# One 2 MB transfer in place of four of 512 KB for each input tile of a graph-layer kernel

## The chip, the core and the metric

The kernel runs on one core of a Trainium2 chip. The profile names the core's engines: PE (matrix multiplication, with its weight loads in a row of their own, PEld), DVE and ACT (elementwise work), POOL (elementwise work and indirect transfers) and SP (which here only issues transfers). Transfers between the chip's memory (DRAM in the code) and the core's on-chip memory are moved by 16 DMA engines. The metric is the device time of one execution in microseconds (us), first to last. Differences of up to about 0.2% (3.9 us here) are what repeated measurements of this kernel cannot tell from nothing.

## The reference: what is computed

For each of 32 batches, x is a 512 x 1024 matrix (channels by nodes) in 32-bit floats. Layer 0 is an attention over the nodes with rank-one scores, layer 1 a plain product with the same 512 x 512 matrix `adj`; each has a residual and a normalization over the last axis:

```python
q = jnp.einsum('c,bcn->bn', wq, x)
k = jnp.einsum('c,bcn->bn', wk, x)
scores = q[:, None, :] + k[:, :, None]
att = jax.nn.softmax(jnp.where(scores > 0, scores, 0.01 * scores), axis=-1)
agg = jnp.einsum('bcn,bmn->bcm', x, att)
x = _layernorm(x + relu(jnp.einsum('oc,bcm->bom', adj, agg) + bm[None, :, None]), axis=-1)
out = _layernorm(x + jnp.einsum('bnf,nm->bmf', x, adj * adj) + bias, axis=-1)
```

## The kernel before, in words

One batch's x is held on chip as a tile of 128 partitions by 4 chunks by 1024 nodes: chunk c holds channels 128c to 128c+127, one to a partition, 4 KB each. `load(b)` (lines 84 to 88) takes a tile from the pool `xp`, which has four buffers, and fills it with four transfers on SP's queue, one for each chunk, of 128 rows of 4 KB. Since there are four buffers, the tile of batch b takes the place of batch b-4, which is still an operand in layer 1 of that batch until its last matrix product and its last DVE combination are done; the first of the four transfers waits for both.

The first reader of a new tile is `parts(b)` (line 247), the products with the two vectors wq and wk. It runs on PE as 16 matrix instructions, chunk by chunk, each with 256 nodes:

```python
for c in range(CT):
    for g in range(CT):
        nc.tensor.matmul(s.ps[32 * g : 32 * g + 32, :], wqk[:, c, :],
            xts[b][:, c, g * Q : (g + 1) * Q], start=(c == 0), stop=(c == CT - 1))
```

The first four of them need chunk 0 alone, the next four chunk 1, and so on. In the profile these are the rows `qk_ps L247`, counted as 32 because each instruction is recorded in two passes. What follows for a batch: the two vectors go to DRAM and come back as a broadcast row (`q_row<-part`, `qb<-q_row`); DVE and ACT count ranks and signs of q against it (`rk` on line 308, `ct` on line 323); PE multiplies x by `adj` (`z_ps` on line 346, and `z_sum_ps` and `z_pair_ps` on line 390, where a two-level scheme saves products); POOL scatters the rows of the product in the order of q to DRAM (`sorted_z`, line 451, eight scatters a batch); they come back (`tab<-sorted_z`, line 470), DVE and ACT make running sums of them, which go out as a table (`table<-tab`, line 553); POOL gathers a row of the table for each node (`got<-table`, line 563); PE turns these (`agg_ps`, line 609), DVE adds the residual into the x tile (line 617), ACT normalizes it, and layer 1 multiplies it (`sum_ps` and `pair_ps`, lines 667 and 702), after which the result is normalized and stored (`out_dram<-g`, line 777).

The order on each engine is written out by hand as a list of words, each a step with its batch: `ld.1` is `load` of the next batch, `pa.1` its `parts`. There is a head for the first batches, a loop that is repeated five times, and a tail. The loop touches five batches at a time, from the next one back to the third before. In the loop, PE's steps between the last product that reads the old tile in its buffer (`12.-3.0`, the pair_ps product of line 667 with S) and `pa.1` are four quarter products (`Y.-3.0`, `Y.-3.1`, `21.-3.0`, `21.-3.1`) and the small `cu.-1` (`carry_ps_True`, line 509). SP issues 16 transfers a batch in the order of the list, each when what it waits for is there: four of x, four of the result, two of `tab`, two of `table`, and four small or broadcast ones. Behind the x transfers in SP's order stands a store of a result chunk. Completion is told through eight semaphores for SP's transfers, taken in turn, so that a transfer also waits for the one eight places before it.

Of the kernel before, what the change touches and what calls it, by code (L numbers as in the profile page):

```python
# [42 lines left out]
P = 128  # L43
# [6 lines left out]
def adj_resnorm_kernel(  # L50
# [10 lines left out]
    nc = tc.nc  # L61
    B, C, N = x.shape
    CT = C // P
# [19 lines left out]

    def load(b):
        t = xp.tile([P, CT, N], F32, tag="x", name=f"x_{b}")
        for c in range(CT):
            nc.sync.dma_start(out=t[:, c, :], in_=x[b, c * P : (c + 1) * P, :])
        xts[b] = t


# [16 lines left out]
    for h in range(2):  # L107
        nc.scalar.dma_start(
            out=room[3 - 3 * h : 6 - 3 * h, 0, :],
            in_=bias[h * H : (h + 1) * H].partition_broadcast(3),  # L110
# [665 lines left out]
    def store(b, m):  # L776
# [5 lines left out]
    ops = {  # L782
        "ldw": adj_load, "wt": adj_turn, "wc": adj_copy_odd, "wd": adj_copy_even, "R": adj_sums,
        "ld": load, "pa": parts, "pc": parts_copy, "co": cols, "cc": cols_copy, "ro": row,
        "tb": top, "tp": top_end, "qw": row_out, "rk": rank, "re": rank_end, "ct": count, "ce": count_end,
        "we": weights_exp, "oq": own_q, "z": product, "zc": product_copy, "sc": scatter,
# [497 lines left out]
```

## Time and profile before

| What | Value |
|---|---|
| median of 3 runs | 1942.26 us (1938.29 to 1942.53) |
| the profiled execution, its own time | 1942.71 us |
| span in its profile | 1940.9 us |
| PE busy | 97% of the span |
| DVE, ACT, POOL busy | 88%, 76%, 46% |
| DMA | 558.05 MB, mean 288 GB/s |
| x transfers | 128 of 512 KB, 0.43 us of SP each (median) |
| granted clock of PE, mean | 0.993 |

The shares are of the span, which runs from the first instruction to the last; the execution's own time is 1.8 us longer. A wait in the profile is named by the instruction that waited and by what ended the wait. The chain is the sequence of work that ended last, followed back from the end: what lengthens a piece of it lengthens the execution. Of the DMA engines the profile has packets (here a packet is mostly one row of a transfer) with queue, start and size: q1 is SP's queue and q0 POOL's.

### The profile page before, as it was taken

To read this page: it belongs to the slowest core of one execution; us is meant where nothing else is said; L and a number is where in the kernel's file an instruction comes from. 1 tells how busy PE (TensorE), PEld (TensorE's weight loads), DVE (VectorE), ACT (ScalarE), POOL (GpSimd) and SP (SyncE) were. 2 spreads that over 40 slices of the span, in tenths; PEclk is the share of its full clock that TensorE was granted. 3 is DMA by queue.
4 is the path that set the end of the run, shared out by engine and by line. 5 is a ranking of instruction groups with operands and counts; after the bars stand their busy time and mean duration, and the time that the engine had idled before them with its cause. 6 is when DMAs were issued, how large, how long until landed. Compare 5 with 4: busy or idle time off the path is not lost.

```text
span 1940.9 us, 23403 instructions
## 1 busy us (share of the span) xinstructions
PE 1887.8 (97%) x7073; PEld 1072.0 (55%) x7073; DVE 1704.6 (88%) x2746; ACT 1483.5 (76%) x2663; POOL 897.2 (46%) x1074
## 2 busy tenths in 40 slices
PE   7988999999999999999999999999999999999897
PEld 3654555555555555566555566555565555554443
DVE  6897899998899889989988989988998989889973
ACT  3566677878778777778787778787777787877786
POOL 5263435335434345454456454455443355445531
PEclk9999999999999999999999999999999999999899
DMA  6577788677888687877787887777888677887862
GB/s 250 197 290 271 286 309 339 253 294 282 313 310 315 252 309 270 331 307 291 290 306 280 317 311 304 277 299 286 308 312 310 262 291 300 308 320 279 331 245 95
DMA packets 147446, 558.05 MB, mean 288 GB/s; under 512 B 19653, under 2 KB 19793, under 8 KB 139129
## 3 DMA queue, kind: packets, MB, share of 16 engines
q1 hardware_dynamic: 89936, 354.40, 48.4%
q0 software_dynamic: 57344, 202.15, 27.6%
q8 instruction: 56, 0.92, 0.2%
q14 instruction: 70, 0.57, 0.1%
q10 hardware_dynamic: 40, 0.02, 0.0%
HBM read 287.08 MB, written 269.42 MB: 287 GB/s over the span
## 4 chain that ended last, share of the span: by engine, by line
PE 78%; DMA 8%; DVE 7%; issue 2%; ACT 2%; POOL 2%; SPq 0%; POOLq 0%; DVEq 0%; ACTq 0%
PE z_ps L346 19%; PE sum_ps L667 18%; PE pair_ps L667 10%; PE z_sum_ps L390 9%; PE z_pair_ps L390 7%; PE pair_ps L702 5%; PE agg_ps L609 4%; DMA table<-tab 3%; PE qk_ps L247 3%; DMA tab<-sorted_z 2%; DVE tab L538 2%; PE carry_ps_True L509 1%; PE carry_ps_False L509 1%; DMA x<-in_x_dram 1%; DMA sorted_z<-zt,to 1%
## 5 line engine op out<-in xcount | busy, mean ns | idle before, releaser
L563 POOL DMA_INDIRECT got<-table,of x256 | 302.3, 1181 | 568.8 <-DMA table<-tab 260.6
L346 PE MATMUL z_ps<-adj_t,x 128*128 128x512 f32 x1088 | 486.9, 594 | 1.4 <-DVE qkc L267 1.1
L451 POOL DMA_INDIRECT sorted_z<-zt,to x256 | 314.0, 1226 | 176.7 <-issue 73.9
L308 DVE SCALAR_TENSOR_TENSOR junk_v<-qb,qkc,tie 128x1024 uint8<-128x1024 f32 x256 | 329.8, 1288 | 10.0 <-DMA qb<-q_row 6.4
L346 PEld LDWEIGHTS z_ps<-adj_t,x 128*128 128x128 f32 x1088 | 202.3, 190 | 225.5 <-issue 212.4
L323 ACT ACTIVATE junk_s<-qb,qkc 128x1024 uint8<-128x1024 f32 x256 | 293.4, 1146 | 19.7 <-DMA qb<-q_row 14.3
L667 PE MATMUL sum_ps<-zt,S 128*128 128x512 f32 x512 | 236.1, 593 | 3.1 <-DVE zt L651 1.4
L585 ACT ACTIVATE got<-got,w 128x512 f32<-128x512 f32 x256 | 172.6, 718 | 42.2 <-DVE w L580 41.8
L590 DVE SCALAR_TENSOR_TENSOR got<-got,w 128x512 f32<-128x512 f32 x256 | 185.6, 746 | 12.0 <-ACT got L585 11.8
L491 DVE SCALAR_TENSOR_TENSOR tab<-tab,ac 128x514 f32<-128x514 f32 x192 | 144.6, 753 | 49.8 <-ACT tab L486 29.2
L617 DVE SCALAR_TENSOR_TENSOR x<-agg_ps,small,x 128x1024 f32<-128x1024 f32 x128 | 163.1, 1280 | 23.9 <-PE agg_ps L609 23.6
L600 ACT ACTIVATE junk<-g,tv 128x1024 uint8<-128x1024 f32 x128 | 146.9, 1148 | 32.9 <-DVE g L722 26.4
L501 DVE SCALAR_TENSOR_TENSOR tab<-tab,ac 128x513 f32<-128x513 f32 x224 | 167.5, 748 | 2.6 <-ACT tab L499 1.9
L667 PEld LDWEIGHTS sum_ps<-zt,S 128*128 128x128 f32 x512 | 96.5, 190 | 121.6 <-issue 105.8
L753 POOL TENSOR_SCALAR tv<-tv 128x1 f32<-128x1 f32 x124 | 53.1, 428 | 238.5 <-ACT junk L600 230.5
L774 ACT ACTIVATE g<-g,nb,tv 128x1024 f32<-128x1024 f32 x124 | 151.0, 1237 | 7.3 <-POOL nb L764 7.2
L600 ACT ACTIVATE junk<-x,tv 128x1024 uint8<-128x1024 f32 x128 | 146.9, 1148 | 12.2 <-DVE x L617 9.9
L538 DVE TENSOR_TENSOR tab<-tab,carry 128x2052 f32<-128x2052 f32 x64 | 146.2, 2291 | 4.7 <-ACT carry L516 4.7
L635 ACT ACTIVATE x<-x,tv 128x1024 f32<-128x1024 f32 x128 | 139.3, 1141 | 0.5
L609 PEld LDWEIGHTS agg_ps<-ident,got 128*128 128x128 f32 x1024 | 116.4, 141 | 36.2 <-issue 24.9
L609 PE MATMUL agg_ps<-ident,got 128*128 128x128 f32 x1024 | 129.4, 274 | 2.7 <-DVE g L722 2.0
L667 PE MATMUL sum_ps<-x,adj 128*128 128x512 f32 x256 | 123.3, 605 | 7.4 <-ACT x L635 7.4
(144 smaller groups left out, 3281.5 us busy)
## 6 DMA issues: line engine op xcount, KB each, us to landing
table<-tab SPq DMA_DIRECT2D x64, 2056.0 KB
tab<-sorted_z SPq DMA_DIRECT2D x64, 1028.0 KB
x<-in_x_dram SPq DMA_DIRECT2D x128, 512.0 KB
out_dram<-g SPq DMA_DIRECT2D x128, 512.0 KB
qb<-q_row SPq DMA_DIRECT2D x32, 512.0 KB
sorted_z<-zt,to POOLq DMA_INDIRECT x256, 5.0
got<-table,of POOLq DMA_INDIRECT x256, 8.0
adj_in<-in_adj_dram SPq DMA_DIRECT2D x1, 1024.0 KB
```

What stands on the lines that cost most here:

```text
L308: nc.vector.scalar_tensor_tensor(s.junk, s.qb, s.q[:, j : j + 1], tie[:, at : at + N], ALU.subtract, ALU.is_gt, accum_out=s.rank[:, j : j ...
L323: nc.scalar.activation(junk, s.qb, AF.Sign, bias=s.k[:, j : j + 1], accum_out=s.sign[:, j : j + 1])
L346: nc.tensor.matmul(s.z[j], xt[:, c, j * P : (j + 1) * P], adj_t[:, c, :], start=(c == 0), stop=(c == CT - 1),)
L390: nc.tensor.matmul(ps, a[:, i, k * P : (k + 1) * P], v[:, i, :], start=start and i == 0 and (k == 0 or bank == 1), stop=(i == 1), skip_gro ...
L451: nc.gpsimd.indirect_dma_start(out=sorted_z[b % 2][:, :], out_offset=bass.IndirectOffsetOnAxis(ap=s.to[:, j : j + 1], axis=0), in_=zt[:, j ...
L538: nc.vector.tensor_tensor(v, v, c, ALU.add)
L563: nc.gpsimd.indirect_dma_start(out=s.got[:, j, :], out_offset=None, in_=table[b % 2][:, :], in_offset=bass.IndirectOffsetOnAxis(ap=s.of[:, ...
L585: nc.scalar.activation(down, down, AF.Copy, scale=s.w[:, 1, j : j + 1])
L590: nc.vector.scalar_tensor_tensor(up, up, s.w[:, 0, j : j + 1], down, ALU.mult, ALU.add)
L600: nc.scalar.activation(junk, t, AF.Square, bias=v[0][:, i : i + 1], scale=-float(N), accum_out=v[1][:, i : i + 1],)
L609: nc.tensor.transpose(s.agg[o][:, j * P : (j + 1) * P], s.got[:, j, o * P : (o + 1) * P], ident)
L667: nc.tensor.matmul(ps, a[:, k, g * P : (g + 1) * P], v[:, k, :], start=False, stop=(k == 1), skip_group_check=first is None,)
```

## The change

Each x tile is filled by one transfer of 2 MB. The tile, its place, the rows of 4 KB and the order of all other steps stay; the transfer has 128 partitions by 4 rows, and there is one completion in place of four. SP issues 13 transfers a batch in place of 16.

```diff
     def load(b):
         t = xp.tile([P, CT, N], F32, tag="x", name=f"x_{b}")
-        for c in range(CT):
-            nc.sync.dma_start(out=t[:, c, :], in_=x[b, c * P : (c + 1) * P, :])
+        nc.sync.dma_start(out=t, in_=x[b].rearrange("(c p) n -> p c n", p=P))
         xts[b] = t
```

## The prediction

> **What bounds the kernel now.** I read the page first. PE is busy nearly all of the span, so only what makes PE wait can move the time. Then the rows by stretches, for the period of the middle batches.
>
> ```profile
> span 1940.9 us, 23403 instructions
> PE 1887.8 (97%) x7073; PEld 1072.0 (55%) x7073; DVE 1704.6 (88%) x2746; ACT 1483.5 (76%) x2663; POOL 897.2 (46%) x1074
> ```
> ```profile
> 934.20:992.43 58.23, 58.23 (x223) 33.67 (x222) 53.07 (x88) 46.76 (x84) 29.36 (x33) 1.00 0.79 299
> 992.43:1050.66 58.23, 58.23 (x223) 33.68 (x222) 52.54 (x86) 46.46 (x84) 29.71 (x33) 1.00 0.80 299
> ```
>
> The columns of the second fence are stretch, length, busy time of PE, PEld, DVE, ACT and POOL, granted clock, DMA share, GB/s. A batch takes 58.23 us there and PE has no gap at full clock: whatever is added to PE's order in this stretch (batches 14 to 25) is added to the time in full.
>
> Third, the order of time around one x load, SP's rows and then PE's.
>
> ```profile
> 934.20 1.77 SPq L87 DMA_DIRECT2D x<-in_x_dram  x4
> 941.15 0.34 SPq L777 DMA_DIRECT2D out_dram<-g  x1
> ```
> ```profile
> 932.67 1.45 PE L667 MATMUL pair_ps<-x,S 128*128 128x512 f32 x3
> 933.96 3.60 PE L667 MATMUL sum_ps<-zt,S 128*128 128x512 f32 x8
> 937.40 3.59 PE L667 MATMUL sum_ps<-zt,adj 128*128 128x512 f32 x8
> 940.83 1.03 PE L509 MATMUL carry_ps_True<-end,before 128*128 128x257 f32 x4
> 941.79 1.93 PE L247 MATMUL qk_ps<-x,wqk 128*32 128x256 f32 x32
> ```
>
> The load is issued when PE ends the last product with the old tile (934.1). PE then has three more steps, and 7.59 us after the first issue (941.79 - 934.20) it starts on the new tile. So this load is not early: PE ties both ends, 7.59 us apart, and the margin does not grow if PE is late.
>
> Fourth, the DMA view: SP's packets from the issue to 941.79, and to 942.4.
>
> ```profile
> q1 hardware_dynamic: 567, 2.07, 82.4%
> ```
> ```profile
> q1 hardware_dynamic: 576, 2.10, 77.1%
> ```
>
> Four loads are 576 packets: 512 rows of 4 KB (2.10 MB), and 64 more, which I take for completions. When PE starts qk_ps, 9 packets have not even begun; the last begins between 942.2 and 942.4. PE does not wait, since chunk 0 is long there and chunk 3 is wanted only after three quarters of 1.93 us, at 943.2. Where the last chunk is really late, the chain shows it.
>
> ```profile
> 408.85 8.04 DMA x<-in_x_dram
> 416.89 0.04 issue
> 416.94 0.64 PE qk_ps L247 x8
> ```
>
> There the last transfer lands at 416.89, the last quarter of qk_ps follows; the view with 576 packets begun is reached between 416.3 and 416.5, so landing comes some 0.4 us after the last packet begins (0.2 to 0.4 by the same reading at 298.86).
>
> **The change part by part.**
>
> Removed: three issues of about 0.43 us a batch. SP issues next a store at 941.15, which waits for ACT, 5 us after; the 1.3 us saved are idle time of SP, and worth nothing. If that cover went, SP would be early, which costs nothing either. With 13 transfers a batch, each still waits for the completion of the one eight places before, now further back in work: no wait is added. In the compiled order nothing else moves on any engine.
>
> Moved: the first four instructions of qk_ps now wait for the whole tile. Queued behind them is all of PE's order, with z_ps next; ACT's copy of qk_ps waits for them, and the row q with it. The price of a batch is (landing of the whole) - (start of qk_ps), where the old order had no wait.
>
> When does one transfer of 2 MB land? No row has it. The nearest in time and rows is the last of the four old ones. It is the same 512 rows on the same queue, and the engines, not the issues, set their pace: issues are 0.47 us apart, 512 KB at the 418 GB/s of a full microsecond (937.20 to 938.20) are 1.25. From one side: in the quickest steady load (817.73) all 576 have begun 7.27 us after the issue, so it lands at 7.7; if one transfer spared the start-up of the later three it could end some 0.4 earlier. From the other: one transfer of 1 MB with four rows a partition (tab, 1433.86) lands 5.42 us after its issue; less 2.6 for its bytes at 400 GB/s leaves 2.8, and 2.8 + 5.2 is 8.0, 0.3 later. The far rows are the 2056 KB writes of the table, 7.6 to 12.1 us in the chain. I take "the same as the last of four", as the nearest, and keep -0.4 to +0.3 for the range. In most batches two scatters of POOL run beside the load and hold it up; they stay.
>
> By the same reading for batches 14 to 25, all packets have begun 1.0, 0, 0.6, 0.6, 0.4, 0.8, 0.4, 0.4, 1.0, 0.8, 0.4, 0.2 us after the start of qk_ps (steps of 0.2): 6.6. With 0.3 for the landing (0.4 less half a step) in eleven and 0.1 in one, 6.6 + 3.4 = 10.0 us, 0.8 a batch.
>
> The early batches: batch 4 0.3, but PE waits 0.9 us some 25 us later for a chain that came off DVE before, so 0; batch 5 0.6 + 0.3 = 0.9; batch 7 0.2; batches 6 and 8 wait for the last chunk today, and there the loss is the three quarters of qk_ps that were done before, 1.93 - 0.64 = 1.29 each. Together 3.7. In batches 9 to 13, 26 to 28 and 30 PE has other work ahead of qk_ps (8.1 to 12.7 us) and all x packets are out: 0. Batches 29 and 31: 575 and 572 packets begun, 0.5 to 0.7 each, 1.3.
>
> The head: today the fourth transfer of x_0 waits 2.5 us for a completion semaphore (SP's waits), is issued at 4.68, and adj behind it at 5.05. Both go out by about 1.7 now. qk_ps of batch 0 ends at 10.45 in the chain; with the whole tile landing 7.7 us after 0.79 and 1.93 of work it is 10.4, so nothing there; but adj is out of the way of x_1 and of the broadcast row behind it, on which DVE waits at 20.9. Between 0 and -1.5; I take -0.7.
>
> Sum: 10.0 + 3.7 + 1.3 - 0.7 = 14.3. Some of the 5 us outside the steady stretch will vanish in gaps that PE has anyway (DVE's chains do not move with the last stall): -1.3. That is +13 on the profiled execution's 1942.71 (span 1940.9 and 1.8 around it), 1955.7; the median of the runs is 0.45 lower, so 1955.3 us, 0.7% slower; a change within 0.2% (3.9 us) could not be told from none.
>
> For the size of a transfer, the trace's rows are 418 GB/s while the 512 KB pieces flow and 7.7 us at best to the landing of the last; by them the sum is the +13 above. The Trainium skill, "DMA: Bandwidth & Descriptors", section "Anatomy of one DMA — SWDGE (gpsimd) path", gives one transfer a fixed 2.0 us and its bytes at 436 GB/s, fitted on POOL's path; that makes an estimate of 6.8 us for 2.10 MB, by which the load would be hidden and the sum about 0. For the number of transfers, the row is the start of qk_ps at 941.79 with 9 packets still to begin. Against this change speaks the page "Perfetto Trace Analysis", section "DMA Optimizations": splitting transfers may let some work start sooner, above all where DMA engines idle (here their share is 0.79); by it one transfer can only lose, and the sum is above 0.
>
> **The rivals.**
> 1. The load is hidden, and the time is the same. It needs the 2 MB to land by +7.59, 0.5 to 1.3 us sooner than the last chunk does in eleven of the twelve steady batches. For it: fewer completions and one start-up, 0.4 at most by the rows above. Time: 14.3 falls to about 0 to 3, 1942 to 1945.
> 2. Faster. If every load, those beside scatters too, lands before qk_ps is reached, the waits on x vanish as well (PE and PEld on DMA x, 1.3 + 4.0 = 5.3 us in all) and the head gives 0.7: -6, 1936. It decides at landings 1.3 us earlier than now; no row has such a gain.
> 3. The four-row form is slow: landing 1 us later than the last chunk. Then the 19 batches that stall pay 1 us more each and some of the others begin to, +33 to +35: about 1976. For it only the 0.3 of the tab row.
> 4. Absorbed: DVE and ACT (88% and 76%) use the stall and PE gains it back at other waits. Against it: PE has no other gap in the steady stretch. If half of the steady 10 and all the rest is gained back, 1947.
>
> **How the numbers follow.** Forecast 0.64 (1948 to 1964: landing -0.4 makes about +6, +0.3 about +19), rival 1 0.14, rival 2 0.05, rival 3 0.09, rival 4 0.08. The range leaves out rival 2 and part of rival 1 below, most of rival 3 above: 1944 to 1969. Slower by over 0.2% (beyond 1946.1): 0.64 + 0.09 + most of rival 4 = 0.80; same 0.15; faster 0.05.
>
> **What would show it.** In the profile after: waits of qk_ps L247 on DMA x, some 25 of 0.2 to 1.3 us, where 9 are now; a steady period of about 59.1 in place of 58.23, with PE's gap at qk_ps alone; the x issue as one row of some 0.4 us; the same mean GB/s over a little more time. Wrong would be: qk_ps without waits in the steady stretch (rival 1), waits of 2 us (rival 3), or new gaps of PE elsewhere.

## The result and the profile after

The changed kernel takes 1959.68 us (median of 6 runs, 1955.97 to 1963.05), the kernel before beside it 1941.47 us (6 runs, 1938.29 to 1942.53). The ratio is 1.0093, with a 95% interval of 1.0083 to 1.0103: slower by 18.2 us. The profiled execution took 1958.28 us, 15.6 us more than the one of before.

Line numbers of after are one lower than before's (qk_ps is L246, the x load L86). In the page of after, the span is longer and the work is the same:

```profile
span 1956.4 us, 23272 instructions
...
PE 1889.3 (97%) x7073; PEld 1077.8 (55%) x7073; DVE 1702.0 (87%) x2746; ACT 1483.2 (76%) x2663; POOL 899.8 (46%) x1074
```

PE is busy 1.5 us more than before in a span that is 15.5 us longer, so some 14 us are new gaps of PE. The rows by stretches show where. I cut both executions at the x issue of batch 14 and at that of batch 26. Columns: stretch, length, busy time of PE, PEld, DVE, ACT and POOL, granted clock, DMA share, GB/s. Before:

```profile
0.00:759.48 759.48, 732.69 (x2794) 421.09 (x2795) 663.94 (x1078) 553.91 (x1003) 343.11 (x424) 1.00 0.76 285
759.48:1459.40 699.92, 699.60 (x2666) 403.54 (x2665) 634.15 (x1020) 556.36 (x994) 347.86 (x396) 1.00 0.79 298
1459.40:1940.87 481.47, 455.48 (x1616) 247.33 (x1614) 406.55 (x651) 373.23 (x668) 206.24 (x254) 0.98 0.72 275
```

After:

```profile
0.00:763.72 763.72, 733.52 (x2794) 422.90 (x2795) 661.10 (x1078) 553.97 (x1003) 347.67 (x424) 0.99 0.75 284
763.72:1472.78 709.06, 700.12 (x2666) 406.43 (x2665) 634.41 (x1020) 556.62 (x994) 352.03 (x396) 1.00 0.78 295
1472.78:1956.44 483.66, 455.62 (x1616) 248.52 (x1614) 406.45 (x651) 372.64 (x668) 200.08 (x254) 0.98 0.72 274
```

The first stretch is 4.2 us longer, the twelve steady batches 9.1, the last 2.2. In the steady stretch PE had 0.3 us without work before and has 8.9 now. Below, "the steady stretch" is always this one, batches 14 to 25, from x issue to x issue.

What PE waits for there is seen in the order of time around one load, SP's row first and then PE's:

```profile
1058.85 0.37 SPq L86 DMA_DIRECT2D x<-in_x_dram  x1
```
```profile
1058.61 3.60 PE L666 MATMUL sum_ps<-zt,S 128*128 128x512 f32 x8
1062.05 3.59 PE L666 MATMUL sum_ps<-zt,adj 128*128 128x512 f32 x8
1065.48 1.03 PE L508 MATMUL carry_ps_True<-end,before 128*128 128x257 f32 x4
1067.43 1.93 PE L246 MATMUL qk_ps<-x,wqk 128*32 128x256 f32 x32 [0.92 <-DMA x<-in_x_dram]
```

This is the picture of before with one thing added: the bracket on the last row. The load is issued as the pair_ps product ends, PE does the same three steps, and would start qk_ps at 1066.5; it stands for 0.92 us until the tile is there. Over the whole execution, the view of PE's waits has this as its longest row, where before had two waits, 1.3 us in all. The columns are us in all, how many, the longest; before first, then after:

```profile
PE qk_ps L247 <- DMA x<-in_x_dram: 1.3, 2, 0.8
```
```profile
PE qk_ps L246 <- DMA x<-in_x_dram: 18.5, 19, 2.7
```

And the chain of work that ended last, which ran through PE alone in this place, now goes through the load (columns: start, length, what). Before, around the load of 934.20, and after:

```profile
934.12 6.87 PE sum_ps L667 x16
940.99 0.87 PE carry_ps_True L509 x4
941.86 1.86 PE qk_ps L247 x32
```
```profile
1055.34 3.45 PE pair_ps L666 x8
1058.79 0.02 SPq L86
1058.81 0.03 issue
1058.85 8.45 DMA x<-in_x_dram
1067.30 0.14 issue
1067.43 1.93 PE qk_ps L246 x32
```

The piece of 8.45 us is the time from the issue to the landing of the 2 MB. The chain has such a piece in eleven of the twelve steady batches: 7.89, 7.78, 8.34, 8.76, 8.45, 8.35, 8.39, 7.70, 8.40, 9.04 and 7.96 us, 8.28 in the mean. These lengths are the loss. Each load is followed by 0.14 us until qk_ps starts, and PE would have started 7.59 us after the issue: the sum over the eleven is 91.06 + 11 x 0.14 - 11 x 7.59 = 9.1 us, and the stretch is 9.1 us longer. That the two agree to the tenth is partly chance: in the twelfth batch (batch 15) qk_ps waits 0.64 us for something else, ACT's reading of the carry product (line 523), and before's own stretch is 1.2 us longer than twelve periods of 58.23 us.

### The profile page after: what moved, and what is told of

The parts are those of the page before. It is cut to its first block, busy times and chain, and to the rows that moved or that the text cites. A ratio compares the mean times of both kernels' runs of the same rounds, so it can differ in the third digit from the quotient of the medians.

```text
span 1956.4 us, 23272 instructions
## 1 busy us (share of the span) xinstructions
PE 1889.3 (97%) x7073; PEld 1077.8 (55%) x7073; DVE 1702.0 (87%) x2746; ACT 1483.2 (76%) x2663; POOL 899.8 (46%) x1074
## 3 DMA queue, kind: packets, MB, share of 16 engines
q1 hardware_dynamic: 88400, 354.39, 47.7%
## 4 chain that ended last, share of the span: by engine, by line
PE 67%; DMA 18%; DVE 6%; ACT 4%; issue 2%; POOL 2%; SPq 0%; DVEq 0%; POOLq 0%; ACTq 0%
PE z_ps L345 19%; PE sum_ps L666 12%; DMA x<-in_x_dram 9%; PE pair_ps L666 9%; PE z_sum_ps L389 8%; PE z_pair_ps L389 6%; DMA tab<-sorted_z 5%; PE pair_ps L701 4%; PE agg_ps L608 4%; DMA table<-tab 3%; PE qk_ps L246 3%; DVE tab L537 2%; PE carry_ps_False L508 1%; DVE got L589 1%; DVE x L616 1%
```

## The experiments

The theory: the four transfers landed just as late, but chunk 0 had landed early and the last chunk was wanted only 1.45 us after qk_ps began (three quarters of its 1.93 us). With one transfer the first instruction waits for the last byte. So the price of a batch is the landing of what an instruction waits for, less the moment at which PE would come to that instruction. The main rival: the wait is no matter of dependence, the single transfer itself is worse (slower, or in the way of others). Each time below is compared with runs of the kernel before made beside it: 1943.02 us (17 runs, 1940.05 to 1945.86) for the reversed order, the two halves, the middle batches and the first of the kernels with a later start; 1945.03 us (17 runs, 1940.74 to 1948.04) for the others.

**Four transfers, but the last one wanted first.** The transfers of before are kept, and qk_ps takes the chunks from 3 down to 0:

```diff
-        for c in range(CT):
+        for c in reversed(range(CT)):
             for g in range(CT):
                 nc.tensor.matmul(
                     s.ps[32 * g : 32 * g + 32, :], wqk[:, c, :],
-                    xts[b][:, c, g * Q : (g + 1) * Q], start=(c == 0), stop=(c == CT - 1),
+                    xts[b][:, c, g * Q : (g + 1) * Q], start=(c == CT - 1), stop=(c == 0),
                 )
```

> The four transfers of 512 KB stay; only qk_ps runs over the chunks backwards (3, 2, 1, 0), so that its first instruction needs the chunk that lands last. Theory (the time goes because PE cannot start qk_ps before the whole 2 MB is there, and one transfer lands when the last of four did): the loss comes back without the single transfer, +14 to +19 us on the kernel before (about 1956 to 1960), some 19 waits of qk_ps on DMA x, 15 to 20 us in all. Rival (the single transfer itself is slower or disturbs the queues): within 3 us of the kernel before, and no more waits than its 9.

Measured: 1963.48 us (1959.62 to 1964.92), ratio 1.0098 (1.0085 to 1.0111), 20 us slower, a little above what was expected. The waits of PE, the steady stretch, and a piece of the chain in this kernel:

```profile
PE qk_ps L247 <- DMA x<-in_x_dram: 21.2, 18, 3.0
```
```profile
767.74:1475.87 708.13, 700.30 (x2666) 405.88 (x2665) 633.82 (x1020) 557.03 (x994) 351.30 (x396) 1.00 0.78 295
```
```profile
1061.27 0.35 SPq L87
...
1062.13 0.43 SPq L87
1062.57 0.04 issue
1062.61 6.64 DMA x<-in_x_dram
1069.25 0.14 issue
1069.38 1.93 PE qk_ps L247 x32
```

The loss is there with four transfers, in the same waits and in the same stretch (8.2 us). Here the fourth transfer is issued at 1062.61, 1.34 us after the first (1061.27), and lands 6.64 us later, 7.98 us after the first issue: within the spread of the single transfer. The eight loads on this kernel's chain in the steady stretch land 7.98 to 8.79 us after their first issue, 8.33 in the mean, against 8.28 for one transfer. The rival falls for the steady stretch: as far as these runs can tell, the size of the transfer does nothing by itself there, and the dependence on the last byte does all of it. Outside it the two kernels differ: the first stretch is 8.3 us longer than before's and the last 5.1, against 4.2 and 2.2 with one transfer.

**Two transfers of 1 MB.**

```diff
-        nc.sync.dma_start(out=t, in_=x[b].rearrange("(c p) n -> p c n", p=P))
+        v = x[b].rearrange("(c p) n -> p c n", p=P)
+        for h in range(2):
+            nc.sync.dma_start(out=t[:, 2 * h : 2 * h + 2, :], in_=v[:, 2 * h : 2 * h + 2, :])
```

> Two transfers of 1 MB for each x, chunks 0 and 1, then 2 and 3. Theory: the second half is wanted only half a qk_ps (0.97 us) after its start, and the last packets come 0.1 to 1.4 us after that start; what is left is 0 to 0.45 us in five of twelve steady batches (1.2 us), 0.3 each in batches 6 and 8, and up to 1 us at the head: +2 to +4 us on the kernel before (about 1944). Rival (time goes with the number or the form of the transfers, with four rows a partition being slow): half of the loss, about +9 us (1950).

Measured: 1942.85 us (11 runs, 1940.72 to 1945.86), ratio 1.0002 (0.9993 to 1.0011). The steady stretch, and what is left of the waits of PE on x:

```profile
758.42:1458.26 699.84, 699.60 (x2666) 403.47 (x2665) 634.03 (x1020) 557.02 (x994) 349.52 (x396) 1.00 0.79 298
```
```profile
PE qk_ps L248 <- DMA x<-in_x_dram: 1.1, 2, 0.8
```

It is the kernel before in time and waits; I had expected a small loss, and missed. Worked from the theory: the second half is wanted 7.59 + 0.96 = 8.55 us after the issue, and of the eleven landings of after only two are later (8.76 and 9.04), by 0.7 us together.

**One of 512 KB and one of 1.5 MB.** Between the two in what it asks: chunks 1 to 3 are wanted after a quarter of qk_ps, 8.07 us after the issue.

```diff
-        nc.sync.dma_start(out=t, in_=x[b].rearrange("(c p) n -> p c n", p=P))
+        v = x[b].rearrange("(c p) n -> p c n", p=P)
+        nc.sync.dma_start(out=t[:, 0:1, :], in_=v[:, 0:1, :])
+        nc.sync.dma_start(out=t[:, 1:CT, :], in_=v[:, 1:CT, :])
```

> Two transfers, of 512 KB (chunk 0) and 1.5 MB (chunks 1 to 3). Theory (the price of a batch is the landing of the last byte less the point of qk_ps that first needs it): that point is a quarter of qk_ps (0.48 us) after its start, so the waits are 0.5 us shorter than with one transfer: about 4.7 us in batches 14 to 25, 0.4 in batch 5, 0.8 each in batches 6 and 8, 0.4 late: +5 to +9 us on the kernel before (1948 to 1952), between one transfer and two halves. Rival (what counts is whether qk_ps can start at all, or the number of transfers): as the two halves, 1941 to 1945.

Measured: 1950.82 us (1949.48 to 1954.48), ratio 1.0038 (1.0024 to 1.0051), 5.8 us slower. The steady stretch, and two batches of the chain:

```profile
758.94:1463.94 705.00, 700.89 (x2666) 402.69 (x2665) 634.55 (x1020) 557.04 (x994) 347.72 (x396) 1.00 0.79 296
```
```profile
1059.68 1.86 PE qk_ps L248 x32
...
1110.64 8.17 DMA x<-in_x_dram
...
1118.86 1.50 PE qk_ps L248 x24
```

The stretch is 5.1 us longer than before's. In the first of these batches qk_ps runs through; in the second its first quarter is done and the chain enters it from the load, so that 24 of the 32 recorded passes follow. The loss grows with the share of qk_ps that must wait for the last byte: +0 for the last half, +5.1 for the last three quarters, +9.1 for all of it (steady stretch).

**One transfer in batches 14 to 25 only.** This asks whether the steady loss adds to the end in full.

```diff
-        nc.sync.dma_start(out=t, in_=x[b].rearrange("(c p) n -> p c n", p=P))
+        if 14 <= b <= 25:
+            nc.sync.dma_start(out=t, in_=x[b].rearrange("(c p) n -> p c n", p=P))
+        else:
+            for c in range(CT):
+                nc.sync.dma_start(out=t[:, c, :], in_=x[b, c * P : (c + 1) * P, :])
```

> One transfer for batches 14 to 25, four for all the others. Theory: in these batches PE has no other gap, so their waits add in full: +8 to +10 us (about 1950), with a PE wait of 0.2 to 1.5 us at qk_ps in each of these twelve and the marks of batches 0 to 13 where they were before. Rival (other engines gain it back, or the loss is made mostly at the head and in the early batches): +4 us or less.

Measured: 1955.99 us (1953.41 to 1958.85), ratio 1.0069 (1.0056 to 1.0082), 13 us slower. The stretches of this kernel:

```profile
0.00:756.26 756.26, 734.09 (x2794) 421.99 (x2795) 662.78 (x1078) 553.94 (x1003) 342.95 (x424) 1.00 0.76 287
756.26:1468.03 711.77, 699.86 (x2666) 406.03 (x2665) 634.08 (x1020) 557.38 (x994) 351.48 (x396) 1.00 0.78 293
1468.03:1951.64 483.61, 455.61 (x1616) 246.41 (x1614) 405.83 (x651) 372.45 (x668) 206.61 (x254) 0.98 0.72 274
```

The twelve batches cost 11.9 us, and none of it is given back later: the last stretch is longer, too, by 2.1 us. The loads of that stretch are those of before, and PE waits for none of them there, so its 2.1 us do not come from a load in it. The 11.9 us are more than after's 9.1 for the same loads; the eleven landings in its chain are 7.90 to 9.27 us, 8.54 in the mean, and 93.93 + 1.54 - 83.49 = 12.0. The median is above the 8 to 10 us that were expected, too. So the price of a batch moves between executions with the landing (0.8 to 1.0 us). The first stretch is a measure for something else: its loads are those of before, and it took 3.2 us less than before's. Differences of some 3 us in the first stretch of single executions say nothing.

**A later start of qk_ps.** If the price is landing less start, then work of PE put ahead of qk_ps must lower it. There is such work: the first `turn` of batch b-3 (agg_ps, line 608 of after, 0.87 us of PE) stands a little behind `pa.1`. It needs three DVE steps (`mix`) earlier. In the loop, one word to a line:

```diff
     mx.-2.5
+    mx.-2.7
+    mx.-2.4
+    mx.-2.0
     d.-1.3
...
-    mx.-2.7
...
-    mx.-2.4
...
     d.-1.1
+    t.-2.2
     pa.1
...
-    mx.-2.0
...
-    t.-2.2
```

It was run three times: with one transfer, for batches 6 and 11 to 26, where in batches 10 and 23 the turn came to stand before three of the mixing steps that it reads, so that those two batches are computed from rows not yet mixed;

> One transfer as in the changed kernel; in PE's order the first turn of the batch three before (agg_ps, 0.87 us) is done before qk_ps in place of after z_ps, for batches 6 and 11 to 26, and DVE's last mixing steps that it needs come ahead of some running sums. Theory (PE's margin of 7.6 us is what the load misses): with 8.5 us most landings (7.8 to 9.0 after the issue) are covered, the waits of qk_ps on DMA x fall from 18.5 us to about 8, and 7 to 9 us come back (about 1951 to 1953). Rival (the load lands late whatever PE does, since its issue hangs on PE): waits and time as in the changed kernel, 1957 to 1961.

with one transfer, for the batches 6, 11, 12 and 14 to 25, in which it stands behind them;

> As the earlier one with the turn ahead of qk_ps, but only for batches 6, 11, 12 and 14 to 25, where the steps that the turn reads are done before it. Theory: the margin in batches 14 to 25 is 8.5 us in place of 7.6 and PE loses less than 2 us there in place of 9; the waits at the head and in batches 5 to 10 stay; 1950 to 1956. Rival (the load lands late whatever PE does): 1957 to 1961 with a PE gap at qk_ps in each of these batches.

and with this order and the four transfers of before:

> The same order of PE and DVE as in the one beside it, with the four transfers of 512 KB. Theory: in the kernel before nothing waits for x in batches 14 to 25, so the order alone gives nothing: 1940 to 1946. Rival (the order itself is worth some us, and that is what came back with one transfer): 1937 or less.

The first took 1957.12 us (1949.56 to 1958.51), ratio 1.0070 (1.0056 to 1.0083), later than the 1951 to 1953 that were expected, though its steady stretch (700.60 us) is only 0.7 us longer than before's; since two of its batches are computed from other rows, the second is used. The second took 1954.34 us (1949.89 to 1959.66), ratio 1.0052 (1.0035 to 1.0068), 9.3 us slower than before in place of 18.2; the third 1946.49 us (11 runs, 1942.99 to 1951.14), ratio 1.0012 (1.0003 to 1.0021), so the order alone gains nothing. The steady stretch of the second and of the third:

```profile
762.28:1464.51 702.23, 699.83 (x2666) 405.83 (x2665) 636.11 (x1019) 555.80 (x994) 328.77 (x396) 1.00 0.78 297
```
```profile
759.34:1459.30 699.96, 699.47 (x2666) 404.81 (x2665) 636.50 (x1020) 556.59 (x994) 331.49 (x396) 1.00 0.79 298
```

With 0.87 us more in front of qk_ps the steady loss falls from 9.1 to 2.3 us (I had expected less than 2). What is left is from landings beyond 7.59 + 0.87 = 8.46 us, and from the 0.14 us that follow them: four loads of this stretch are on the chain, with 8.60, 9.49, 8.65 and 9.05 us, which by the same sum make 2.5. The loss of the first and of the last stretch remains.

**The scatters out of the load's way.** Two of POOL's eight scatters a batch run beside each load. This kernel has one transfer and puts these two behind the load (POOL's order only), to ask how much of the landing is due to them. In the loop, one word to a line:

```diff
     r1.-3.1
-    sc.0.1
     21.-3.0
...
     s1.-3.0
-    sc.0.0
     mx.-2.5
...
     r1.-3.3
+    sc.0.1
+    sc.0.0
```

> One transfer as in the changed kernel; for the loads of batches 14 to 25 the two scatters that POOL issues beside the load (of the batch before) come behind the last statistics steps of POOL, some 8 us later. Theory (the load takes 7.6 to 7.9 us alone, and what it needs beyond is the two scatters' 0.6 us each on the same DMA engines): landings in these batches fall from 7.7-9.0 us after the issue to 7.6-8.0, the waits of qk_ps there from about 10 us to about 3, and 5 to 8 us come back (1951 to 1955), unless the later scatters make the loads of the sorted rows wait. Rival (the spread of landings has another cause): landings as before, no time back.

Measured: 1982.13 us (1974.43 to 1982.32), ratio 1.0183 (1.0165 to 1.0201), 37 us slower: a miss. The two scatters came some 12 us later (960.67 and 962.07, for a load issued at 945.87), and the steady stretch is 731.22 us. What was expected of the load itself did come: in this stretch qk_ps waits for x six times, 2.8 us in all, against eleven times and 8.3 us in after, and the six loads on its chain landed a little earlier (7.72, 7.76, 8.05, 8.77, 7.90 and 7.67 us, 7.98 in the mean, against 8.28). But other work became late, and cost more. One piece of the chain:

```profile
989.20 1.26 POOL sorted_z L450
990.76 7.38 DMA sorted_z<-zt,to
998.23 1.23 DVE zt L655
1000.12 1.32 DVE got L589 x2
1002.69 0.75 DVE tab L500
1004.16 1.75 ACT got L584 x3
1005.91 8.77 DMA x<-in_x_dram
```

DVE's layer-1 sum on line 655 writes into the one tile `zt` that the scatters read from. Here a scatter's transfer ends just before that sum, and the x load comes behind the sum and what DVE and ACT do after it. This is one piece; PE's waits in the stretch are spread over several places (pair_ps on ACT's g of line 711, 6.0 us, is the largest), and why these became late isn't shown. So the run's time doesn't price the scatters.

The trace of after says more about them. Of its eleven loads, the four beside which the second scatter began more than 5 us after the issue (batches 14, 16, 22 and 25) landed after 7.70 to 7.96 us, the seven where it began after 4.51 us or less after 8.34 to 9.04 us. With one transfer in the middle batches only, three of four such loads landed after 7.90 to 8.08 us and one after 9.27, the seven others after 8.30 to 9.13. With four transfers and the reversed order there is no such split. So in the trace of after the moment of the scatters goes with 0.7 us of the landing (7.83 us in the mean of the four, 8.53 of the seven), but that they cause it isn't shown, and with none beside it a load still took 8.77 us.

## Why the prediction was right, and where it was off

The predicted time was 1955.3 us, the measured one 1959.68. The mechanism is shown: the wait, its place, and that it adds in full. Term by term, in the two profiled executions (the differences outside the steady stretch from the ends of qk_ps of the same batch in both traces):

| Term of the sum | predicted, us | measured, us |
|---|---|---|
| head, to batch 4 | -0.7 | +0.55 |
| early batches, 5 to 13 | 3.7 | 3.7 |
| steady batches, 14 to 25 | 10.0 | 9.1 |
| batches 26 to 28 | 0 | 0.1 |
| batches 29 to 31 | 1.3 | 2.3 |
| given back elsewhere | -1.3 | -0.2 |
| sum | 13 | 15.6 |

*"It lands as the last of the four did"* was right. It was taken from the nearest row, with -0.4 to +0.3 kept open; the fourth transfer of the kernel with the reversed order shows the same landing, and the twelve batches cost 9.1 us where 10.0 had been read off the packets. Two things moved it, one down and one up: the landings were earlier than read, and 0.14 us pass between landing and the first matrix instruction, which the working didn't have. The sum held and the single batches did not, so part of the fit is luck: batch 22 lost 0.25 us where 1.3 was said, batch 24 1.6 where 0.7 was said. In the execution with one transfer in the middle alone it was 11.9. The term's own spread, from the landings of one execution to the next, is about as large as the bounds I had given to the unknown. And those bounds were added up wrongly at the top: +19 on 1942 is 1961, not the 1964 of the forecast.

*"Some of the 5 us will vanish in gaps that PE has anyway: -1.3"* was wrong. Nothing was given back: the run with one transfer only in the middle ended with its whole steady loss, and 0.2 us is all that the pair of traces shows. There is no row in the profile of before for such a gain; it was a guess from the length of the gaps.

*The head, -0.7,* had the wrong sign, by little. The working had qk_ps of batch 0 end at 10.4, from a landing 7.7 us after the issue and 1.93 us of work. In the trace of after it is:

```profile
8.93 3.29 PE L246 MATMUL qk_ps<-x,wqk 128*32 128x256 f32 x32 [1.93 <-DMA x<-in_x_dram]
```

The load took 8.00 us, and the first qk_ps lasts 3.29 us. That could be read in the profile of before, whose chain has 3.67 us for it; I took the duration of the steady rows. x_1 is so issued at 13.35 in place of 11.52. Most of this is lost in waits that were there, and 0.55 us is left at batch 4. Given that the first stretch of the same loads took 756.3 and 759.5 us in two executions, that term and the early one can't be tested much closer; that the early sum fits is partly chance, since batch 7 lost 1.0 where 0.2 was said, batch 8 0.3 where 1.29 was said, and batch 10 0.6 where nothing was said: its load took 10.96 us, longer than PE's other work covered.

*Batches 29 and 31* had 1.3 for the two; batches 29 to 31 lost 0.5, 0.5 and 1.3. Only the last two waited for x (0.43 and 0.93 us), batch 29 for ACT. Since the kernel with one transfer in the middle alone has the same 2.1 us more in its last stretch without any such wait, this term can't be put down to the loads with confidence.

*The issues saved on SP* were worth nothing, as said: one row of 0.37 us in place of four, and no row of SP starts a chain sooner. The q1 packets fell from 89936 to 88400, by 48 a tile, which bears out that the 64 packets over the 512 rows were completions (16 to a transfer).

*The rivals.* That the load is hidden, and that the kernel becomes faster: no, eleven of twelve steady batches wait. That the form with four rows a partition lands 1 us later: no, the landings agree with those of four transfers. That the stall is absorbed: no, by the run of the middle alone. The predicted signs in the profile: 19 waits of qk_ps on x where "some 25" were said, up to 1.5 us in the steady stretch where 1.3 was the bound, and longer ones before it (1.93 for x_0, 2.65 for x_1, 2.27 for x_6); a steady period of 709.06 / 12 = 59.1 us, as said.

The estimate of 6.8 us that the prediction worked out from the Trainium skill, "DMA: Bandwidth & Descriptors", section "Anatomy of one DMA — SWDGE (gpsimd) path", doesn't hold for this queue with this work beside it: 7.70 to 9.04 us were measured. What the Trainium skill's page "Perfetto Trace Analysis", section "DMA Optimizations", says of splitting held, with the DMA share at 0.78, and not only where the engines idle.

What stays open: the medians lie 18.2 us apart and the two profiled executions 15.6; I haven't shown where the other 2.6 are, though the steady stretch alone differs by 2.7 us between two executions with the same loads in it. That the scatters hold the load up, as the prediction had it, rests on the split in two traces told above; how much of the landing they cause is open as well. A fifth x tile, with which the load would start a batch earlier, wasn't tried.

## What to carry to other kernels

Before transfers are merged, write down for each piece when its first reader comes to it, counted from the issue, and when the last byte lands; a merged transfer makes all its readers wait for the last byte, and the price is the landing less the time at which the first of them would have started. Here four transfers and one brought the last byte of the same 2 MB equally late, so the cut decides: two halves cost nothing (1.0002), a quarter and three quarters 0.4%, the whole 0.9%. If an issue is tied to the same engine that reads the tile, as here by the buffer that PE frees, the margin is a constant of the order of work, and each batch pays again.

## What was not expected of the hardware

- One transfer of 2 MB and four of 512 KB land together, although the four are issued over 1.3 us: 7.98 to 8.79 us after the first issue for the last of four (reversed order), 7.70 to 9.04 for one, in the steady stretch. SP needs no longer to issue the large one (0.37 us; 0.43 for one of 512 KB).
- Landings of the same load in the same order of work differ by 1.3 us within one execution, and their mean by 0.26 us between two (8.28 and 8.54).
- The first qk_ps takes 3.29 us and a matrix instruction of it up to 636 ns, against 1.93 us and 379 ns later. In the second (21.15, 2.89 us) the profile shows a granted clock of 0.65 (from 21.10 to 24.10); in the first it shows 1.00. So the clock row does not account for the first, and what does is open.
- Two scatters moved back by some 12 us on POOL, an engine that is 46% busy, made the kernel 19 us slower than the whole change did. On the piece of chain shown, DVE's sum waits for a scatter that reads the tile it writes, and the next x load comes after it; the rest of that loss is open.
